# The mask of one attention added by four quarters of TensorE's array, with half of the heads' keys exchanged

## The chip, the cores and the metric

The kernel runs on one core of a Trainium2 chip. The metric is the device time of one execution in microseconds (us). Before the change it is 3333.31 us, the median of three runs (3326.55 to 3346.01). The profile quoted here is of one execution by itself, which took 3340.76 us.

The engines are named as the profile names them: PE is TensorE (matrix products; PEld are its weight loads), DVE is VectorE, ACT is ScalarE, POOL is GpSimd, SP is SyncE, which here issues the DMAs. PSUM is the memory that PE writes; L1050 means line 1050 of the kernel.

## The reference

Two transformer layers on one sequence `x` of 2048 rows by 256 columns, with 16 heads of 16 columns. The first layer has self attention inside each half of the sequence, cross attention between the halves, and an MLP. The second has self attention under a mask over all 2048 keys, cross attention to a context of 1601 rows, and an MLP. Cut to the attention that matters here:

```python
def _mha(q_in, k_in, v_in, qw, qb, kw, kb, vw, vb, ow, ob, mask):
    q = (q_in @ qw + qb).reshape(b, sq, NHEAD, hd).transpose(0, 2, 1, 3)
    k = (k_in @ kw + kb).reshape(b, sk, NHEAD, hd).transpose(0, 2, 1, 3)
    v = (v_in @ vw + vb).reshape(b, sk, NHEAD, hd).transpose(0, 2, 1, 3)
    scores = jnp.einsum('bhqd,bhkd->bhqk', q, k) / jnp.sqrt(jnp.float32(hd))
    if mask is not None:
        scores = jnp.where(mask == 0, jnp.float32(-1000000000.0), scores)
    attn = jax.nn.softmax(scores, axis=-1)
    out = jnp.einsum('bhqk,bhkd->bhqd', attn, v)
    return out.transpose(0, 2, 1, 3).reshape(b, sq, d) @ ow + ob
```

`_mha` runs first with the integer mask (2048 by 2048), then with the context and no mask.

## The kernel before

There are four attention stages, `st` 0 to 3; `st == 2` is the masked one. Queries go by blocks of 512 (`BLK`), heads by groups `g` of four. One group of one block is a unit. Of its four heads two belong to `h` = 0 and two to `h` = 1. In the tiles of keys `kT` and of queries `q` the heads of `h` = 0 lie on partitions 0 to 63 and those of `h` = 1 on 64 to 127, so the score products of the two halves use two different halves of the array's rows. Keys are in slots of 1024 columns, each of eight tiles of 128 keys.

A unit is worked in two passes. The first (`maxima`, L957, L965, L972) computes scores with queries on the partitions and keys along 512 columns, and takes each row's maximum. In the masked stage DVE adds the mask to the scores while it takes the maximum (L965, one instruction for each `h`, followed by a read of its accumulator). The maxima are negated, split into two parts (`negated`) and turned into rows `nm` (`as_rows`, L996).

The second pass (`weights_of`) computes scores with 128 keys on the partitions and 512 queries along the columns (L1035), adds minus the maximum by another pair of products (L1042), and in the masked stage adds the mask, transposed (`bias_columns`, made by `mask_columns` with transposes on PE, L925), by a product with a unit matrix `ident16` (L1050). All three accumulate in one PSUM tile `s_ps` of two banks, a bank for each `h`; ACT then takes the exponential of both banks (L1055). `values_of` multiplies the weights `e` with the values `V`, four heads on four column strips of the array (L1072). `V` has for each key 17 numbers for each head, in the order of the keys.

Both passes take their PSUM tiles from one pool of three (`big_ps`), in turn. The maxima of a unit are computed while the weights of the unit before it are; in the masked stage each step therefore has one pair of products of the maxima, one of weights, and one group of L1072. What else there is to do (MLP, projections, keys and values of the next stage) is cut into pieces and put between the steps by `after` and `evict`. The order of instructions on every engine is the order in which the program issues them (`manual_schedule`). SP issues all DMAs in order: a DMA that waits holds up those behind it. `load_ready` issues one waiting transfer of keys or values a step.

Keys, queries and values are computed once a block (`halves`, `values`). `halves` splits each product in a rounded part `hi` (ACT, L439) and the rest `lo` (DVE, L440), and stores both to DRAM (L444); `c` is the `h` of the heads, `w` is 1 for keys. `values` stores one tile of values by one DMA (L487). The loads back are L809 (keys), L823 (values) and L868 (queries).

Of the kernel before, what the change touches and what calls it, by code (L numbers as in the profile page):

```python
# [12 lines left out]
F32 = mybir.dt.float32  # L13
# [3 lines left out]
AF = mybir.ActivationFunctionType  # L17
ALU = mybir.AluOpType
# [4 lines left out]
P = 128  # L23
# [3 lines left out]
NG = 4  # L27
# [13 lines left out]
GW = 4 * VW  # L41
# [35 lines left out]
def two_layers(ctx: ExitStack, tc: tile.TileContext, a: dict, out: bass.AP):  # L77
    nc = tc.nc
# [74 lines left out]
    ident16 = sb.tile([P, P], BF16, tag="ident16", name="ident16")  # L153
# [37 lines left out]
    def half(shape, dtype=F32, name="half"):  # L191
        return sb.tile(shape, dtype, tag="half", bufs=3, name=name)
# [74 lines left out]
    src = a["cols"][:, :32].rearrange("(c i r) (t w g) -> g i c r t w", c=2, i=2, t=4, w=2)  # L267
    qkb_loads = []
    for g in range(NG):
        for i in range(2):  # L270
            at = (2 * g + i) * HD
# [19 lines left out]
    m = one_ps()  # L291
# [40 lines left out]
    m = one_ps()  # L332
# [48 lines left out]
    def transposed(src, n=BLK, mod=None, tag="hT"):  # L381
# [31 lines left out]
            yield from piece(lambda m, k=k: turn(m, k), lambda m, k=k: take(m, k))  # L413
        return hT

    def halves(st, w, hT, b, n):

        wqk = weights[st][0]
        if w:
            slot = 0 if b in KEYS[st][0] else 1  # L420
            at = KEYS[st][slot].index(b) * BLK
            if (st, slot) not in keys_dr:
                keys_dr[st, slot] = dr.tile([2, 2, P, SLOT], F32, tag="k", bufs=8, name="k_dr")
            d = keys_dr[st, slot][:, :, :, at : at + BLK]
        else:
            d = queries_dr[st, b] = dr.tile(
                [2, 2, P, BLK], F32, tag="q", bufs=4 * NB, name="q_dr"
            )

        def product(m, c):  # L430
            for k in range(2):
                nc.tensor.matmul(  # L432
                    m[:, :n], lhsT=wqk[:, k, w, c, :], rhs=hT[:, k, :n], start=k == 0, stop=k == 1
                )

        def split(m, c):
            hi, lo = half([P, BLK], F32R, name="hi"), half([P, BLK], F32R, name="lo")
            bias = qkb[:, st, w, c : c + 1]
            nc.scalar.activation(hi[:, :n], m[:, :n], AF.Identity, bias=bias)  # L439
            nc.vector.scalar_tensor_tensor(  # L440
                lo[:, :n], m[:, :n], bias, hi[:, :n].bitcast(F32), ALU.add, ALU.subtract
            )
            for i, t in enumerate((hi, lo)):
                nc.sync.dma_start(d[c, i, :, :n], t[:, :n].bitcast(F32))  # L444

        for c in range(2):
            yield from piece(lambda m, c=c: product(m, c), lambda m, c=c: split(m, c))
        if not w:
            done.add(("q", st, b))

    def values(st, hT, b, n):
        _, wv, bv = weights[st]
        t = stage([P, TPB, H * VW], name="v")
        by_head = t.rearrange("p t (h d) -> p t h d", h=H)
        nc.gpsimd.memset(by_head[:, :, :, HD:], 1.0)
        d = dr.tile([P, TPB, H * VW], F32, tag="v", bufs=4 * NB, name="v_dr")
        spans = [(i, min(P, n - i * P)) for i in range((n + P - 1) // P)]

        def product(m, two):
            for j, (i, r) in enumerate(two):  # L460
                for k in range(2):
                    nc.tensor.matmul(  # L462
                        m[:r, j * D : (j + 1) * D], lhsT=hT[:, k, i * P : i * P + r],
                        rhs=wv[:, k, :], start=k == 0, stop=k == 1,
                    )

        def add(m, two):
            full = [i for i, r in two if r == P]
            rest = [i for i, r in two if r < P]
            for r, ii, j in ((P, full, 0), (two[-1][1], rest, len(full))):  # L470
                if ii:
                    nc.vector.tensor_tensor(
                        by_head[:r, ii[0] : ii[0] + len(ii), :, :HD],
                        m[:r, j * D : (j + len(ii)) * D].rearrange(
                            "p (t h d) -> p t h d", t=len(ii), h=H
                        ),
                        along(bv[:r], len(ii), r).rearrange("p t (h d) -> p t h d", h=H),
                        ALU.add,
                    )

        for i in range(0, len(spans), 2):
            two = spans[i : i + 2]
            yield from piece(
                lambda m, two=two: product(m, two), lambda m, two=two: add(m, two)
            )
        full = n // P
        nc.sync.dma_start(d[:, :full, :], t[:, :full, :])  # L487
        if n % P:
            nc.sync.dma_start(d[: n % P, full, :], t[: n % P, full, :])
        values_dr[st, b] = d  # L490

    def keys_and_values(st, hT, b, n=BLK):
        yield from halves(st, 1, hT, b, n + n % 2)
# [438 lines left out]
    def maxima(u):  # L932

        st, b, g = u["st"], u["b"], u["g"]
        masked = st == 2
        chunks = []
        for slot in u["slots"]:
            nk = slot_rows(st, slot)
            n = -(-nk // BLK)
            size = -(-nk // n)  # L940
            size += size % 2
            nk += nk % 2
            chunks += [(slot, c, min(size, nk - c)) for c in range(0, nk, size)]

        def pair(qt, n, i):
            if "pm" not in u:
                load_needed("keys", u)
                u["pm"] = sb.tile([P, TPB, 2, 2, len(chunks)], F32, tag="pm", bufs=2, name="pm")
            if masked and i == 0 and g == NG - 1 and 1 in u["slots"]:
                at = ORDER[2].index(b) + 1  # L950
                each = 2 * 2 // len(chunks)
                for j in range(n * each, (n + 1) * each) if at < NB else ():
                    mask_rows(ORDER[2][at], j // 2, qt, j % 2)
            slot, c, nn = chunks[n]
            s = big_ps()
            for h in range(2):
                nc.tensor.matmul(  # L957
                    s[:, h, :nn],
                    lhsT=u["q"][64 * h : 64 * h + 64, i, qt * P : (qt + 1) * P],
                    rhs=kT[g][slot][64 * h : 64 * h + 64, i, c : c + nn],  # L960
                    start=True, stop=True,
                )
            if masked:
                for h in range(2):
                    nc.vector.tensor_tensor_reduce(  # L965
                        out=s[:, h, :], in0=s[:, h, :],
                        in1=bias_rows[b, slot, qt][:, c : c + nn],
                        scale=1.0, scalar=-3.0e38, op0=ALU.add, op1=ALU.max,
                        accum_out=u["pm"][:, qt, h, i, n : n + 1],
                    )  # L970
            else:
                nc.vector.tensor_reduce(u["pm"][:, qt, :, i, n], s[:, :, :nn], AX.X, ALU.max)  # L972

        return [
            lambda qt=qt, n=n, i=i: pair(qt, n, i)
            for qt in range(TPB) for n in range(len(chunks)) for i in range(2)
        ]
# [43 lines left out]
    def weights_of(u):  # L1021

        st, b, g = u["st"], u["b"], u["g"]
        masked = st == 2
        u["tiles"] = [
            (slot, kt, min(P, slot_rows(st, slot) - kt * P))
            for slot in u["slots"] for kt in range(-(-slot_rows(st, slot) // P))
        ]
        u["e"] = {}

        def pair(n, i):
            slot, kt, r = u["tiles"][n]
            s = big_ps()
            for h in range(2):
                nc.tensor.matmul(  # L1035
                    s[:r, h, :],
                    lhsT=kT[g][slot][64 * h : 64 * h + 64, i, kt * P : kt * P + r],
                    rhs=u["q"][64 * h : 64 * h + 64, i, :],
                    start=True, stop=False,
                )  # L1040
            for h in range(2):
                nc.tensor.matmul(  # L1042
                    s[:r, h, :],
                    lhsT=sel[64 * h : 64 * h + 64, i, :r],
                    rhs=u["nm"][64 * h : 64 * h + 64, :],
                    start=False, stop=not masked,
                )
            if masked:
                for h in range(2):
                    nc.tensor.matmul(  # L1050
                        s[:, h, :], lhsT=ident16, rhs=bias_columns[b, slot, kt],
                        start=False, stop=True,
                    )
            e = u["e"][n, i] = sb.tile([P, 2, BLK], F32, tag="e", bufs=EB, name="e")
            nc.scalar.activation(e[:r], s[:r], AF.Exp, scale=SCALE)  # L1055

        return [lambda n=n, i=i: pair(n, i) for n in range(len(u["tiles"])) for i in range(2)]
# [395 lines left out]
```

## Time and profile before

| what | value |
|---|---|
| median of three runs | 3333.31 us |
| the profiled execution | 3340.76 us |
| its span, first to last instruction | 3338.9 us |
| granted clock of PE over the span | 0.969 |
| mask products, L1050 | 1024, from 1230.2 to 2441.8 us |
| products of the maxima, L957 | 3072, of which 1024 in the masked stage |
| mask and maximum on DVE, L965 | 1024, 701 ns each, and a read of 142 ns |

In rows of groups the columns are line, engine, operation, out<-in with shapes, count, then busy us and the mean ns of one, then idle time of the engine before them and what ended most of it. In the chain of waits each piece has its start, its length, the engine, what it writes and its line. In the timeline the idle time of the engine before a row and its releaser stand in brackets. A tile shape such as 64*128 means 64 rows and 128 columns of the array. The end of a product is modelled.

### The profile page before, as it was taken

To read this page: it belongs to the slowest core of one execution; us is meant where nothing else is said; L and a number is where in the kernel's file an instruction comes from. 1 tells how busy PE (TensorE), PEld (TensorE's weight loads), DVE (VectorE), ACT (ScalarE), POOL (GpSimd) and SP (SyncE) were. 2 spreads that over 40 slices of the span, in tenths; PEclk is the share of its full clock that TensorE was granted. 3 is DMA by queue.
4 is the path that set the end of the run, shared out by engine and by line. 5 is a ranking of instruction groups with operands and counts; after the bars stand their busy time and mean duration, and the time that the engine had idled before them with its cause. 6 is when DMAs were issued, how large, how long until landed. Compare 5 with 4: busy or idle time off the path is not lost.

```text
span 3338.9 us, 56839 instructions
## 1 busy us (share of the span) xinstructions
PE 3054.3 (91%) x22592; PEld 1371.8 (41%) x22592; DVE 2164.9 (65%) x3925; ACT 1718.1 (51%) x1892; POOL 404.0 (12%) x344
## 2 busy tenths in 40 slices
PE   5889999999998989898999999999989999999995
PEld 2434444444444435343433343343344444444433
DVE  4666777775656566566777777777667757666541
ACT  1455565565555545443545555555556546545461
POOL 0001101101011122113013013010010010110102
PEclk8899999999999999999999999999999999999997
DMA  6462251260216121343012011003230100001000
GB/s 171 131 118 80 63 98 58 72 114 26 66 33 116 31 79 42 95 117 101 27 39 59 20 39 52 13 22 70 49 87 27 27 17 21 26 17 27 11 14 16
DMA packets 162363, 191.21 MB, mean 57 GB/s; under 512 B 82584, under 2 KB 95520, under 8 KB 162096
## 3 DMA queue, kind: packets, MB, share of 16 engines
q1 hardware_dynamic: 162096, 187.57, 22.8%
q8 instruction: 178, 2.92, 0.4%
q14 instruction: 89, 0.73, 0.1%
HBM read 129.91 MB, written 48.46 MB: 53 GB/s over the span
## 4 chain that ended last, share of the span: by engine, by line
PE 59%; DVE 6%; ACT 4%; DMA 3%; SPq 2%; issue 2%; POOL 1%; ACTq 0%; POOLq 0%; DVEq 0%
PE m_ps L1072 15%; PE s_ps L1035 10%; PE s_ps L957 9%; PE s_ps L1050 7%; PE s_ps L1042 6%; ACT e L1055 3%; PE m_ps L565 3%; PE m_ps L618 3%; DVE s_ps L965 2%; DVE pm L972 1%; PE m_ps L507 1%; PE m_ps L432 1%; DMA kT<-k_dr 1%; PE m_ps L462 1%; DVE t L375 1%
## 5 line engine op out<-in xcount | busy, mean ns | idle before, releaser
L1055 ACT ACTIVATE e<-s_ps 128x1024 f32<-128x1024 f32 (+1 forms) x1440 | 1466.9, 1024 | 1330.7 <-PE s_ps L1042 739.4
L972 DVE TENSOR_REDUCE pm<-s_ps 128x2 f32<-128x1024 f32 (+3 forms) x1024 | 1122.5, 1107 | 512.2 <-PE s_ps L957 508.9
L1072 PE MATMUL m_ps<-e,V 128*32 128x256 f32 (+2 forms) x10432 | 909.7, 420 | 1.0 <-DVE lo L440 0.8
L965 DVE CUSTOM_DVE_ANT_0 s_ps<-s_ps,bias 128x512 f32<-128x512 f32 x1024 | 713.2, 701 | 286.7 <-PE s_ps L957 147.4
L957 PE MATMUL s_ps<-kT,q 64*128 64x512 f32 (+3 forms) x3072 | 655.5, 428 | 112.4 <-ACT e L1055 63.9
L1035 PE MATMUL s_ps<-q,kT 64*128 64x512 f32 (+1 forms) x2880 | 681.6, 469 | 45.0 <-ACT e L1055 24.7
L1042 PE MATMUL s_ps<-nm,sel 64*128 64x512 f32 (+1 forms) x2880 | 576.2, 395 | 0.0
L957 PEld LDWEIGHTS s_ps<-kT,q 64*128 64x128 f32 x3072 | 295.4, 187 | 475.2 <-issue 244.1
L1035 PEld LDWEIGHTS s_ps<-q,kT 64*128 64x128 f32 (+1 forms) x2880 | 271.5, 185 | 506.9 <-issue 286.6
L1072 PEld LDWEIGHTS m_ps<-e,V 128*32 128x32 f32 (+1 forms) x10432 | 207.2, 109 | 442.6 <-issue 420.7
L1050 PE MATMUL s_ps<-biasT,ident 128*128 128x512 bf16 x1024 | 311.0, 385 | 0.0
L1150 POOL TENSOR_TENSOR oT<-oT,rd_rows 64x512 f32<-64x512 f32 x64 | 81.6, 1275 | 1873.6 <-DMA rd_rows<-rd_dr 1540.2
L1042 PEld LDWEIGHTS s_ps<-nm,sel 64*128 64x128 f32 (+1 forms) x2880 | 277.0, 188 | 10.3 <-ACT nm L1001 0.5
L902 POOL TENSOR_SCALAR bias<-raw 128x512 bf16<-128x512 int32 x64 | 123.0, 1923 | 275.5 <-DMA raw<-in_mask 264.1
L965 DVE DVE_READ_ACCUMULATOR2_ANT pm<- 128x1 f32 x1024 | 145.3, 142 | 0.0
L1050 PEld LDWEIGHTS <-ident 128*128 128x128 bf16 x1024 | 58.3, 97 | 186.4 <-issue 186.4
L432 PE MATMUL m_ps<-hT,w_qk 128*128 128x512 f32 (+2 forms) x224 | 106.6, 599 | 10.4 <-DVE lo L440 7.7
L565 PE MATMUL m_ps<-hT,w_mlp 128*128 128x512 f32 x224 | 110.4, 616 | 5.7 <-ACT sums L1104 4.4
L440 DVE SCALAR_TENSOR_TENSOR lo<-m_ps,qkb,hi 128x512 fp32r<-128x512 f32 (+2 forms) x56 | 41.1, 734 | 109.7 <-ACT hi L439 66.0
L618 PE MATMUL m_ps<-w_mlp,hid 128*128 128x256 f32 x448 | 104.6, 387 | 0.0
L618 PEld LDWEIGHTS m_ps<-w_mlp,hid 128*128 128x128 f32 x448 | 83.9, 191 | 19.3 <-issue 8.5
L462 PE MATMUL m_ps<-w_v,hT 128*128 128x256 f32 (+1 forms) x244 | 63.8, 407 | 25.6 <-DVE lo L440 22.6
(107 smaller groups left out, 1278.0 us busy)
## 6 DMA issues: line engine op xcount, KB each, us to landing
q<-q_dr SPq DMA_DIRECT2D x544, 64.0 KB
kT<-k_dr SPq DMA_DIRECT2D x192, 128.0 KB
raw<-in_mask SPq DMA_DIRECT2D x64, 256.0 KB
q_dr<-hi SPq DMA_DIRECT2D x32, 256.0 KB
q_dr<-lo SPq DMA_DIRECT2D x32, 256.0 KB
oT<-sums SPq DMA_DIRECT2D x256, 32.0 KB
rd_rows<-rd_dr SPq DMA_DIRECT2D x64, 128.0 KB
v_dr<-v SPq DMA_DIRECT2D x14, 544.0 KB
```

Source lines behind the costliest of these rows:

```text
L432: nc.tensor.matmul(m[:, :n], lhsT=wqk[:, k, w, c, :], rhs=hT[:, k, :n], start=k == 0, stop=k == 1)
L565: nc.tensor.matmul(m, lhsT=w1[k][:, f * P : (f + 1) * P], rhs=hT[:, k, :], start=k == 0, stop=k == 1,)
L618: nc.tensor.matmul(m[:, q2 * D : (q2 + 1) * D], lhsT=hid[f][:, qt * P : (qt + 1) * P], rhs=w2[f // 4][:, f % 4, :], start=f == 0, stop=f = ...
L902: nc.gpsimd.tensor_scalar(bias_rows[b, slot, qt][:, j * BLK : (j + 1) * BLK], raw, 0.0, MASKED, ALU.is_equal, ALU.mult,)
L957: nc.tensor.matmul(s[:, h, :nn], lhsT=u["q"][64 * h : 64 * h + 64, i, qt * P : (qt + 1) * P], rhs=kT[g][slot][64 * h : 64 * h + 64, i, c : ...
L965: nc.vector.tensor_tensor_reduce(out=s[:, h, :], in0=s[:, h, :], in1=bias_rows[b, slot, qt][:, c : c + nn], scale=1.0, scalar=-3.0e38, op0 ...
L972: nc.vector.tensor_reduce(u["pm"][:, qt, :, i, n], s[:, :, :nn], AX.X, ALU.max)
L1035: nc.tensor.matmul(s[:r, h, :], lhsT=kT[g][slot][64 * h : 64 * h + 64, i, kt * P : kt * P + r], rhs=u["q"][64 * h : 64 * h + 64, i, :], st ...
L1042: nc.tensor.matmul(s[:r, h, :], lhsT=sel[64 * h : 64 * h + 64, i, :r], rhs=u["nm"][64 * h : 64 * h + 64, :], start=False, stop=not masked,)
L1050: nc.tensor.matmul(s[:, h, :], lhsT=ident16, rhs=bias_columns[b, slot, kt], start=False, stop=True,)
L1055: nc.scalar.activation(e[:r], s[:r], AF.Exp, scale=SCALE)
L1072: nc.tensor.matmul(u["av"][PH * j : PH * (j + 1), cut], lhsT=V[g][slot][:r, kt * GW + j * VW : kt * GW + j * VW + PH], rhs=u["e"][n, j % 2 ...
```

## The change

In the masked stage the mask is added by four products instead of two. Each uses 64 rows and 64 columns of the array: for `h` = 0 the upper and the lower half of the tile of keys go straight (rows 0 to 63 to columns 0 to 63, and 64 to 127 to 64 to 127), for `h` = 1 crossed. For that, the scores of `h` = 1 have the two halves (64 keys each) of every tile of 128 keys exchanged. The exchange is made where keys and values of that stage are stored: `split` writes the keys of `c` = 1 through `exchanged` in two parts, and `values` stores with three DMAs, one for the heads of `h` = 0 and two for those of `h` = 1. In the maxima the mask is in plain order, so there the product of `h` = 1 is made by two products of 256 columns that exchange the keys back.

```diff
+    def exchanged(t, h):
+        return t.rearrange("p (t h x) -> p t h x", h=2, x=P // 2)[:, :, h, :]
...
         def split(m, c):
-            nc.scalar.activation(hi[:, :n], m[:, :n], AF.Identity, bias=bias)
-            nc.vector.scalar_tensor_tensor(
-                lo[:, :n], m[:, :n], bias, hi[:, :n].bitcast(F32), ALU.add, ALU.subtract
-            )
+            if st == 2 and w and c:
+                parts = [(exchanged(m, h), exchanged(hi, 1 - h), exchanged(lo, 1 - h)) for h in range(2)]
+            else:
+                parts = [(m[:, :n], hi[:, :n], lo[:, :n])]
+            for x, high, low in parts:
+                nc.scalar.activation(high, x, AF.Identity, bias=bias)
+                nc.vector.scalar_tensor_tensor(
+                    low, x, bias, high.bitcast(F32), ALU.add, ALU.subtract
+                )
...
+        values_dr[st, b] = d
+        if st == 2:
+            src, dst = (x.rearrange("p t (g c) -> p (t g) c", g=NG) for x in (t, d))
+            nc.sync.dma_start(dst[:, :, : GW // 2], src[:, :, : GW // 2])
+            for at in (0, P // 2):
+                nc.sync.dma_start(
+                    dst[P // 2 - at : P - at, :, GW // 2 :], src[at : at + P // 2, :, GW // 2 :]
+                )
+            return
         nc.sync.dma_start(d[:, :full, :], t[:, :full, :])
...
             for h in range(2):
-                nc.tensor.matmul(
-                    s[:, h, :nn],
-                    lhsT=u["q"][64 * h : 64 * h + 64, i, qt * P : (qt + 1) * P],
-                    rhs=kT[g][slot][64 * h : 64 * h + 64, i, c : c + nn],
-                    start=True, stop=True,
-                )
+                queries = u["q"][64 * h : 64 * h + 64, i, qt * P : (qt + 1) * P]
+                keys = kT[g][slot][64 * h : 64 * h + 64, i, c : c + nn]
+                if masked and h:
+                    for part in range(2):
+                        nc.tensor.matmul(
+                            exchanged(s[:, h, :], part), lhsT=queries,
+                            rhs=exchanged(keys, 1 - part), start=True, stop=True,
+                        )
+                    continue
+                nc.tensor.matmul(s[:, h, :nn], lhsT=queries, rhs=keys, start=True, stop=True)
...
-            if masked:
-                for h in range(2):
-                    nc.tensor.matmul(
-                        s[:, h, :], lhsT=ident16, rhs=bias_columns[b, slot, kt],
-                        start=False, stop=True,
-                    )
+            for h, half_ in ((0, 0), (0, 1), (1, 0), (1, 1)) if masked else ():
+                to, of = 64 * half_, 64 * (half_ ^ h)
+                nc.tensor.matmul(
+                    s[to : to + 64, h, :],
+                    lhsT=ident16[of : of + 64, of : of + 64],
+                    rhs=bias_columns[b, slot, kt][of : of + 64, :],
+                    start=False, stop=True,
+                )
```

More of the change, by code (lines that the diff above doesn't have):

```diff
@@ L489, in values @@
             nc.sync.dma_start(d[: n % P, full, :], t[: n % P, full, :])
-        values_dr[st, b] = d
     def keys_and_values(st, hT, b, n=BLK):
```

## The prediction

> **What bounds the kernel now.** I read the busy table first, then the groups, then the chain of waits and the timeline inside the masked stage. All times are of one profiled execution: span 3338.9 us, its own time 3340.8 us, 0.2% above the median 3333.3 us of the three runs.
>
> ```profile
> PE 3054.3 (91%) x22592; PEld 1371.8 (41%) x22592; DVE 2164.9 (65%) x3925; ACT 1718.1 (51%) x1892; POOL 404.0 (12%) x344
> ```
>
> TensorE is busy 91%. The groups that the change touches or has as neighbours, from the page (line, engine, tile, count, then busy us and mean ns):
>
> ```profile
> L1072 PE MATMUL m_ps<-e,V 128*32 128x256 f32 (+2 forms) x10432 | 909.7, 420 | 1.0 <-DVE lo L440 0.8
> L965 DVE CUSTOM_DVE_ANT_0 s_ps<-s_ps,bias 128x512 f32<-128x512 f32 x1024 | 713.2, 701 | 286.7 <-PE s_ps L957 147.4
> L957 PE MATMUL s_ps<-kT,q 64*128 64x512 f32 (+3 forms) x3072 | 655.5, 428 | 112.4 <-ACT e L1055 63.9
> L1035 PE MATMUL s_ps<-q,kT 64*128 64x512 f32 (+1 forms) x2880 | 681.6, 469 | 45.0 <-ACT e L1055 24.7
> L1050 PE MATMUL s_ps<-biasT,ident 128*128 128x512 bf16 x1024 | 311.0, 385 | 0.0
> ```
>
> Line 1050 is the addition of the mask: 1024 products, two to a step, so 512 masked steps, between 1230 and 2442 us. One such step in the chain of waits of a quiet stretch (start us, us, engine and line):
>
> ```profile
> 2002.38 0.57 PE m_ps L1072 x8
> 2002.95 0.42 PE s_ps L957 x2
> 2003.38 0.26 PE s_ps L1035 x2
> 2003.64 0.23 PE s_ps L1042 x2
> 2003.86 0.54 PE s_ps L1050 x2
> 2004.40 0.57 PE m_ps L1072 x8
> 2004.97 0.43 PE s_ps L957 x2
> 2005.40 0.23 PE s_ps L1035 x2
> ```
>
> The step is five pieces of TensorE work end to end: 0.57 + 0.43 + 0.23 + 0.23 + 0.54 = 2.00 us, and 0.03 more when the L1035 piece is 0.26. The pair of L957 and the pairs of L1035 and L1042 run side by side on the two halves of the rows (each pair takes one stream of 512 columns, 0.23); the two products of L1050 use all rows and follow each other (0.54 = two streams of about 0.22 and about 0.1 around them). What the 0.26 is, the timeline of the same steps tells:
>
> ```profile
> 2002.88 0.19 PEld L957 LDWEIGHTS s_ps<-kT,q 64*128 64x128 f32 x2 [0.41 <-issue]
> 2002.94 0.14 DVE L965 DVE_READ_ACCUMULATOR2_ANT pm<- 128x1 f32 x1
> 2003.13 0.19 PEld L1035 LDWEIGHTS s_ps<-q,kT 64*128 64x128 f32 x2
> 2003.53 0.70 DVE L965 CUSTOM_DVE_ANT_0 s_ps<-s_ps,bias 128x512 f32<-128x512 f32 x1 [0.45 <-ACT e L1055]
> ...
> 2004.94 0.14 DVE L965 DVE_READ_ACCUMULATOR2_ANT pm<- 128x1 f32 x1
> 2005.13 0.19 PEld L1035 LDWEIGHTS s_ps<-q,kT 64*128 64x128 f32 x2
> ```
>
> The weight load of L1035 starts 0.05 us after the DVE read of the maxima ends (2003.08 to 2003.13, 2005.08 to 2005.13): three `s_ps` buffers serve maxima and weights in turn, and L1035 writes the one that DVE has just left. So there is a second loop, over two steps: DVE from its start to its end 1.55 (3.53 to 5.08), 0.05 to the load of L1035, 1.77 from there through L1042, L1050 and L1072 to the L957 after next (5.13 to 6.90), 0.65 from that to the next DVE start. 1.55 + 0.05 + 1.77 + 0.65 = 4.02, or 2.01 a step. TensorE alone (2.00) and this loop (2.01) bind together.
>
> **The mask addition, part by part.** Two products with all rows become four on 64 rows and 64 columns, one on each quarter. If the four stream together, the piece is one stream instead of two. The stream and what surrounds it come from the starts of weight loads: after the first load of L1050, a following load of the same tile shape (line 925) comes at 0.23, as soon as the second stream begins, but that of L1072 at 0.54; so ending the last stream and changing the shape costs 0.54 - 0.23 - 0.22 = about 0.09. Ahead of the stream stands the weight load. For quarter loads no row exists; the nearest are the 128x32 loads of L1072 (load to first column about 0.03: first products last 0.40, later ones 0.38) and the 64x128 loads of L957 (about 0.11: 0.49 against 0.38). I take 0.05 to 0.06, between them in columns. New piece: 0.06 + 0.22 + 0.09 = 0.37 plus 0.01 for four starts (the starts of L1072's four column tiles are 0.006 apart) = 0.38. Saving 0.16 a step. Ends: 0.20 saved if the load is as short as L1072's or shorter; 0.05 lost if only two quarters stream at a time (0.59); 0.48 lost if each goes alone (1.02). I take the first because L1072 shows four column tiles together and L957 two row tiles together.
>
> **The maxima.** For the second half of heads one product of 512 columns becomes two of 256 with the same weights, so 512 extra loads on that row half. The other half still streams 512 columns. First load 0.11, 256 columns 0.11, the second load behind it 0.11, then 256 columns: ready at about 0.34 against 0.33. The nearest row for short products with their own loads is L996 (128 columns): four loads and products start 0.11 apart, so a load hides behind a short product. Taken: +0.01; ends 0 and +0.11 (second load not hidden). DVE waits for the last of the three, so this lies in the DVE loop too.
>
> **A moved wait.** In the changed order of instructions the first L1035 product (line 1061 there) waits for DVE and also for an earlier PE product; the latter is the maxima product that DVE itself waited for, so it is long done, but with two waits the DVE wait becomes an instruction of its own on TensorE's queue. Before shows such ones:
>
> ```profile
> L957 PEldq EVENT_SEMAPHORE x38: 51/51/51, 1747.7 to 2370.6; - x38
> ```
>
> Behind it stand L1035, L1042, the mask and L1072, all in order. Price: 0.05 per step where DVE arrives last, nothing where it is early (TensorE is still streaming L957); ends 0 and 0.11, the distance of two such waits in a row.
>
> **Around them.** Four key splits become two ACT and two DVE instructions of 256 columns in place of one of 512 (0.69 and 0.75 now): under 0.5 us each, four times, beside PE work. Four stores of values turn from one DMA of 128 pieces into three of 4096 pieces of 136 B in all. Their issue on SP:
>
> ```profile
> L823 SPq DMA_DIRECT2D V<-v_dr x64: 387/598/1531, 79.9 to 2473.4; - x64
> L487 SPq DMA_DIRECT2D v_dr<-v x16: 320/338/1192, 73.9 to 1581.1; - x16
> ```
>
> 512 pieces take 0.60, 128 take 0.34: about 0.7 ns a piece more, so about 3.6 us for the three against 0.34. The last of these stores (1359.6) is followed on SP by `kT` loads for which PE waits 8.5 us until 1381.3; between lies a wait of SP for the row maxima until 1371.2, which should swallow the 3 us. Price of all this +3, ends 0 and +13 (four times 3.3, uncovered).
>
> **Sum.** Read from the starts of the mask pairs in order of time, 140 of the gaps between neighbours are over 2.4 us: steps with MLP, projection or other background products on PE (the chain there is TensorE alone, with 1.72 of line 565 in a step of 3.72). The other 372 are quiet steps of 2.0 to 2.2, in most of which the load of L1035 follows DVE by 0.05.
> Quiet: the DVE loop crosses the mask once in two steps: 4.02 - 0.16 + 0.01 + 0.05 = 3.92, 1.96 a step; TensorE alone would be 2.00 - 0.16 + 0.01 = 1.85. DVE's loop wins: gain 0.05 (0.045 unrounded) x 372 = 17 us.
> Heavy: 0.16 - 0.01, and something for waits = 0.137 x 140 = 19 us.
> 17 + 19 - 3 = 33 us: 3340.8 becomes 3308 for a profile of that kind, and the median 3333.3 becomes 3300.
>
> [...] L1035's row tiles write two different banks, L1072's column tiles four partition groups of one bank; no row here has tiles of different rows in one bank. [...]
>
> **Rivals.** (1) Quarters take turns, two at a time: the piece is 0.59, quiet steps lose (0.05 + 0.06) / 2 = 0.06, heavy ones 0.07: 22 + 10 + 3 = +35, 3368. It speaks for it that no row shows four quarters; against, that rows and columns each split well. It decides as soon as the piece exceeds 0.48 (0.38 plus twice the 0.045 that a quiet step gains). Each alone (1.02): (0.48 + 0.06) / 2 x 372 + 0.49 x 140 + 3 = +172, 3505.
> (2) The second load of the maxima is exposed: +0.11 instead of +0.01: quiet steps get 4.02 - 0.16 + 0.11 + 0.05 = 4.02, no gain; heavy ones 0.05 x 140 = 7, less the 3; 3330. Against it stands L996.
> (3) DVE does not bind, because the score products finish in time in both steps or the wait hides: all 512 steps gain 0.14, 70 us, 3266. Against it: 4.02 is added up from four readings that each repeat within 0.02.
>
> **How the numbers follow.** About 0.5% (17 us) can be told from no change. Forecast 0.50 (3290 to 3318), rival 3 0.12, rival 2 with near-nothing outcomes 0.14, rival 1 0.16, slower than that 0.08. Faster by over 0.5%: 0.12 and nearly all of the 0.50, 0.60. Same: 0.16. Slower: 0.24. The range takes in rivals 1 to 3 and leaves out several turns: 3266 to 3368.
>
> **What would show it.** Right: the mask's four products start within 0.03 us of each other and the piece is 0.35 to 0.40; the load of line 1061 follows DVE by about 0.1; quiet steps 1.94 to 1.98, heavy ones 0.14 shorter. Wrong: a mask piece over 0.5; the second maxima product ending 0.1 later; a longer PE gap near 1381 (stores); quiet steps at 1.86 (DVE not binding).

## The result: no change that can be told

After the change the kernel takes 3336.38 us (median of 12 runs, 3329.84 to 3349.09); the kernel before takes 3335.36 us in 12 runs beside it. The ratio is 1.0003, 95% interval 0.9989 to 1.0017. A gain of about 1% was forecast and none came. The profiled execution took 3341.12 us with a span of 3339.3 us, against 3338.9 us before, so the two profiles can be laid over each other.

The mask itself became cheaper. From the busy table and the groups of the kernel after (line, engine, tile, count, busy us and mean ns; L1076 is the mask, L983 the pairs of short products in the maxima of `h` = 1):

```profile
PE 3021.9 (90%) x24128; PEld 1410.7 (42%) x24128; DVE 2164.9 (65%) x3929; ACT 1720.4 (52%) x1896; POOL 404.2 (12%) x344
...
L983 PE MATMUL s_ps<-kT,q 64*128 64x256 f32 x1024 | 252.9, 329 | 9.0 <-DMA kT<-k_dr 8.4
L1076 PE MATMUL s_ps<-biasT,ident 64*64 64x512 bf16 x2048 | 211.3, 403 | 0.0
```

PE is busy 32 us less (3021.9 against 3054.3), in the same span. The chain of waits of the kernel after, in a quiet stretch of the masked stage, shows two steps (L988 is the product of the maxima of `h` = 0, L1061 the scores of the weights):

```profile
2007.91 0.34 PE s_ps L1076 x4
...
2008.83 0.32 PE s_ps L988
2009.14 0.14 PE s_ps L983
...
2009.31 0.50 PE s_ps L1061 x2
...
2010.05 0.34 PE s_ps L1076 x4
...
2011.40 0.23 PE s_ps L1061 x2
...
2011.86 0.34 PE s_ps L1076 x4
```

The mask piece is 0.34 us instead of 0.54: the four quarters run side by side. From one mask to the next is 2.14, then 1.81 us, a mean of 1.97 where it was 2.01. The long step is the one in which L1061 takes 0.50 instead of 0.23. Its weight load, in the timeline of the kernel after, stands behind the DVE read of the maxima:

```profile
2009.02 0.14 DVE L991 DVE_READ_ACCUMULATOR2_ANT pm<- 128x1 f32 x1
2009.28 0.21 PEld L1061 LDWEIGHTS s_ps<-q,kT 64*128 64x128 f32 x2 [0.23 <-PE s_ps L983]
```

The read ends at 2009.16 and the load starts at 2009.28, about 0.12 later, where it was 0.05 before.

So the stage that was changed did gain. From the first to the last mask load it takes 1196.3 us instead of 1211.4. But that first load comes at 1246.9 us instead of 1230.2: the 15.1 us won are lost ahead of the stage, 16.7 us. The ends of the units (the copies of their sums on ACT) tell where. Counted from 0 and against before, unit 21 ends 3.2 us earlier; then units 22, 26 and 30 fall back by 8.2, 10.7 and 5.1 us, each in one jump, and unit 34 by 2.3; between them some 5 us are won back, and no other jump is over 2.6 us. In exactly these four units the stores of values are issued (851.9, 1016.3, 1200.5 and 1375.6 us). At the first of them the chain of waits of the kernel after has one long piece:

```profile
855.27 8.50 DMA q_dr<-hi
...
863.96 0.76 DVE lo L453
...
864.77 0.66 PE m_ps L1022 x4
```

Around it, PE by stretches of 4 us (window, its length, PE busy and instructions, granted clock, mean busy share of the DMA engines, GB/s), kernel after:

```profile
848.00:852.00 4.00, 4.00 (x30) 0.94 0.00 0
852.00:856.00 4.00, 3.95 (x24) 1.00 0.91 89
856.00:860.00 4.00, 3.91 (x26) 1.00 1.51 73
860.00:864.00 4.00, 1.00 (x10) 1.00 0.97 177
864.00:868.00 4.00, 3.23 (x22) 0.69 0.19 69
868.00:872.00 4.00, 4.00 (x36) 0.89 0.20 60
```

and the kernel before, three of the same stretches:

```profile
852.00:856.00 4.00, 4.00 (x28) 1.00 0.36 143
856.00:860.00 4.00, 3.90 (x24) 1.00 0.35 133
860.00:864.00 4.00, 4.00 (x42) 1.00 0.35 131
```

Before, the 128 pieces of the store, of 4352 bytes each, start between 853.4 and 854.7 us in the DMA records, and the stretch that holds them has a share of 0.36. After, the 4096 pieces of 136 bytes start between 853.2 and 860.1 us, at shares of 0.91 and 1.51 and at 89 and 73 GB/s instead of 143 and 133. (The share adds up the times of all pieces; it is over 1 where they overlap.) The store of queries `q_dr<-hi`, issued behind them at 855.27, lands 8.50 us later (in the kernel before it is issued at 855.92, and the last of its pieces and of the `lo` behind it starts at 858.3). Until then DVE may not write a new `lo`, because `hi` and `lo` come from a pool of three buffers (`half`); the products that make the rows `nm` (L1022) wait for this `lo`, and the next unit's weights need `nm`. PE is busy 1.00 of 4 us, and afterwards the granted clock is 0.69 and 0.89 for two windows, by estimate up to 1.7 us more ((0.31 + 0.11) x 4).

### The profile page after: what moved, and what is told of

Same layout as the page of the kernel before. It is cut to its first block, busy times and chain, and to the rows that moved or that the text cites. A ratio compares the mean times of both kernels' runs of the same rounds, so it can differ in the third digit from the quotient of the medians.

```text
span 3339.3 us, 60415 instructions
## 1 busy us (share of the span) xinstructions
PE 3021.9 (90%) x24128; PEld 1410.7 (42%) x24128; DVE 2164.9 (65%) x3929; ACT 1720.4 (52%) x1896; POOL 404.2 (12%) x344
## 4 chain that ended last, share of the span: by engine, by line
PE 58%; DVE 7%; ACT 4%; DMA 3%; issue 2%; SPq 2%; POOL 1%; ACTq 0%; DVEq 0%; POOLq 0%
PE m_ps L1100 15%; PE s_ps L1061 11%; PE s_ps L988 7%; PE s_ps L1068 6%; PE s_ps L1076 4%; ACT e L1083 4%; PE m_ps L587 3%; PE m_ps L640 3%; DVE s_ps L991 3%; PE s_ps L983 2%; PE m_ps L529 1%; DVE pm L998 1%; DMA q_dr<-hi 1%; PE m_ps L475 1%; PE m_ps L439 1%
## 5 line engine op out<-in xcount | busy, mean ns | idle before, releaser
L1061 PE MATMUL s_ps<-q,kT 64*128 64x512 f32 (+1 forms) x2880 | 694.5, 475 | 60.9 <-ACT e L1083 24.5
L988 PE MATMUL s_ps<-kT,q 64*128 64x512 f32 (+3 forms) x2560 | 651.4, 415 | 103.1 <-ACT e L1083 63.9
L1068 PE MATMUL s_ps<-nm,sel 64*128 64x512 f32 (+1 forms) x2880 | 584.0, 396 | 0.0
L1061 PEld LDWEIGHTS s_ps<-q,kT 64*128 64x128 f32 (+1 forms) x2880 | 300.3, 185 | 523.3 <-issue 302.1
L988 PEld LDWEIGHTS s_ps<-kT,q 64*128 64x128 f32 x2560 | 292.9, 187 | 462.8 <-issue 229.5
L1068 PEld LDWEIGHTS s_ps<-nm,sel 64*128 64x128 f32 (+1 forms) x2880 | 284.4, 188 | 2.5 <-ACT nm L1027 0.2
L983 PE MATMUL s_ps<-kT,q 64*128 64x256 f32 x1024 | 252.9, 329 | 9.0 <-DMA kT<-k_dr 8.4
L1076 PE MATMUL s_ps<-biasT,ident 64*64 64x512 bf16 x2048 | 211.3, 403 | 0.0
L983 PEld LDWEIGHTS s_ps<-kT,q 64*128 64x128 f32 x1024 | 152.8, 186 | 11.0 <-issue 10.2
L1076 PEld LDWEIGHTS <-ident 64*64 64x64 bf16 x2048 | 57.9, 103 | 187.5 <-issue 187.5
L453 DVE SCALAR_TENSOR_TENSOR lo<-m_ps,qkb,hi 128x512 fp32r<-128x512 f32 (+3 forms) x60 | 42.0, 699 | 135.6 <-ACT hi L452 64.3
L587 PE MATMUL m_ps<-hT,w_mlp 128*128 128x512 f32 x224 | 111.1, 618 | 5.8 <-ACT sums L1132 4.4
```

What stands on the lines that cost most here:

```text
L587: nc.tensor.matmul(m, lhsT=w1[k][:, f * P : (f + 1) * P], rhs=hT[:, k, :], start=k == 0, stop=k == 1,)
L983: nc.tensor.matmul(exchanged(s[:, h, :], part), lhsT=queries, rhs=exchanged(keys, 1 - part), start=True, stop=True,)
L988: nc.tensor.matmul(s[:, h, :nn], lhsT=queries, rhs=keys, start=True, stop=True)
L1061: nc.tensor.matmul(s[:r, h, :], lhsT=kT[g][slot][64 * h : 64 * h + 64, i, kt * P : kt * P + r], rhs=u["q"][64 * h : 64 * h + 64, i, :], st ...
L1068: nc.tensor.matmul(s[:r, h, :], lhsT=sel[64 * h : 64 * h + 64, i, :r], rhs=u["nm"][64 * h : 64 * h + 64, :], start=False, stop=not masked,)
L1076: nc.tensor.matmul(s[to : to + 64, h, :], lhsT=ident16[of : of + 64, of : of + 64], rhs=bias_columns[b, slot, kt][of : of + 64, :], start= ...
```

## Experiments

All ratios are to the kernel before, run beside the experiment on the same chip. A difference in us is that of the two medians, so it can deviate a little from the ratio, which comes from all runs.

### The stores alone: `store_only`

The kernel before, with only the three stores of `values` from the change (the keys are not exchanged, so half of the heads meet the wrong values).

```diff
+        if st == 2:
+            src, dst = (x.rearrange("p t (g c) -> p (t g) c", g=NG) for x in (t, d))
+            nc.sync.dma_start(dst[:, :, : GW // 2], src[:, :, : GW // 2])
+            for at in (0, P // 2):
+                nc.sync.dma_start(
+                    dst[P // 2 - at : P - at, :, GW // 2 :], src[at : at + P // 2, :, GW // 2 :]
+                )
+            return
```

> The kernel before with the changed store of the masked stage's values alone (three DMAs of 136-byte pieces; keys are not exchanged, so the values of half of the heads meet the wrong keys). Theory S (the stores ate the gain: in the changed kernel the ends of units 22, 26 and 30, each in the time of such a store, are late by 8.2, 10.7 and 5.2 us, of which 16.5 stand at the start of the masked stage): 14 to 20 us slower than before, ratio 1.004 to 1.006, the same three jumps. Theory N (the lag is chance, the masked stage gives nothing): ratio 1.000.

3362.03 against 3335.29 us, ratio 1.0092 (1.0077 to 1.0107): 27 us. The jumps are at the same units: 6.2 us at 22, 7.9 at 26, 7.5 at 30, 3.2 at 34. The waits between 845 and 880 us name the same chain (engine, line and what was waited for: us in total, times, longest):

```profile
DVE lo L440 <- DMA q_dr<-hi: 7.4, 1, 7.4
PEld m_ps L1006 <- DVE lo L440: 4.8, 1, 4.8
```

The stores alone cost more than the change lost, and more than was expected; nothing of the mask is needed for it. Why it is 27 us here and 18 in the changed kernel (next experiment) was not separated.

### The change without its stores: `plain_store`

The kernel after with the one store of before (so the values of half of the heads are not exchanged).

```diff
-        if st == 2:
-            src, dst = (x.rearrange("p t (g c) -> p (t g) c", g=NG) for x in (t, d))
-            nc.sync.dma_start(dst[:, :, : GW // 2], src[:, :, : GW // 2])
...
-            return
```

> The changed kernel with one DMA a block for the values, in the order of the keys (the values of half of the heads are left unexchanged). Theory S: 14 to 20 us faster than before, ratio 0.994 to 0.996, no jumps at units 22, 26, 30. Theory N: ratio 1.000, as the changed kernel.

3318.03 against 3335.29 us, 0.9955 (0.9939 to 0.9972). The units 22 to 34 end within about 2 us of where they end before, and the first mask load comes at 1230.1. So the rest of the change is worth 17 us and the stores take 18 of them.

### The two products and their wait alone: `two_products`

The kernel before, with the maxima of the second half of heads by two products of 256 columns, in plain order.

```diff
-                nc.tensor.matmul(
-                    s[:, h, :nn],
...
+                for x in (0, 256) if masked and h else (None,):
+                    y = slice(0, nn) if x is None else slice(x, x + 256)
+                    nc.tensor.matmul(s[:, h, y], lhsT=queries, rhs=keys[:, y], start=True, stop=True)
```

> The kernel before, with the second half's product of the maxima in two of 256 columns, which also brings the separate instruction that waits for DVE. Keys, values and mask as before. If the wait costs 0.05 us in the DVE loop over two steps and the product 0.01: quiet steps 2.04 instead of 2.01, 372 of them, 8 to 14 us slower, ratio 1.003 to 1.004. If the wait is hidden: ratio 1.000.

3345.95 against 3335.29 us, 1.0037 (1.0024 to 1.005): 11 us. The groups of L1034 (the scores of the weights in this kernel) show the wait as an instruction of its own:

```profile
L1034 PEldq EVENT_SEMAPHORE  x444: 51/51/51, 1189.2 to 2383.5; - x148
```

The kernel before has none there, the kernel after 443 of the same length. In the chain the two products of the maxima (L961) take 0.43 or 0.44 us, as the pair did before, which leaves the wait as what costs: the load of L1034 now starts 0.11 to 0.12 us behind the end of DVE's read in 290 of the 512 steps, where 278 steps of the kernel before have 0.04 to 0.06.

### Values exchanged on PE, maxima by one product: `both`

The kernel after, with both costs removed and the result kept. The values are exchanged when PE makes them: the products for the heads of `h` = 1 write their 64 keys to the other half of the partitions, and the tile is stored by one DMA. The maxima of `h` = 1 are one product whose keys are read with a negative step over the two halves.

```diff
+                    for h, at in ((0, 0), (0, 64), (1, 64), (1, 0)):
+                        to = at if h == 0 else 64 - at
+                        for k in range(2):
+                            nc.tensor.matmul(
+                                y[to : to + 64, :, h, :], lhsT=hT[:, k, i * P + at : i * P + at + 64],
+                                rhs=w[:, k, :, h, :], start=k == 0, stop=k == 1,
+                            )
...
-                    for part in range(2):
...
+                    keys = keys.rearrange("p (t h x) -> p t h x", h=2, x=P // 2)[:, :, ::-1, :]
```

> The changed kernel with the values exchanged where they are computed (products of 64 keys to exchanged partitions, one DMA a block) and the maxima of the second half by one product whose keys are read with a step backwards, so that neither the small pieces nor the extra product nor its wait is there. Theory S: stores give back 17, wait and product 372 x 0.03 = 11, on top of the changed kernel's time; less some 4 us for the value products: 20 to 30 us faster than before, ratio 0.991 to 0.994. Theory N: ratio 0.997 at best, from the wait alone.

3299.28 against 3335.29 us, 0.9895 (0.9881 to 0.991): 36 us faster, more than the 20 to 30 expected. In its chain of waits the maxima are one pair again (L985), and the mask (L1073) is what it was in the kernel after:

```profile
2009.15 0.07 DVE pm L988
2009.22 0.04 issue
2009.26 0.50 PE s_ps L1058 x2
...
2010.90 0.43 PE s_ps L985 x2
...
2011.79 0.34 PE s_ps L1073 x4
```

The scores (L1058) follow the end of DVE by 0.04. The long quiet steps lie mostly between 1.99 and 2.03 us, in the kernel after between 2.08 and 2.16; the short ones are 1.78 to 1.83 in both.

From the first to the last mask load it needs 1173.3 us, 38 less than before, and its first load comes at 1227.4.

### One at a time: `values_pe` and `one_product`

`values_pe` has only the first half of the diff above, `one_product` only the second.

> The changed kernel with the values of the masked stage exchanged where they are computed and stored by one DMA a block; the extra product of the maxima and its wait stay. As plain_store (0.9955) plus 0 to 5 us for the smaller value products: ratio 0.995 to 0.998. If the small products cost more on TensorE than the stores did: ratio 1.000 or over.

> The changed kernel with the maxima of the second half by one product, its keys read with a step backwards, so without the extra product and the separate wait; the stores in small pieces stay. If the wait is worth in the changed kernel what two_products showed against before (12 us): 8 to 16 us faster than before, ratio 0.995 to 0.998. If it is hidden there: ratio 1.000.

`values_pe`: 3319.02 against 3335.39 us, 0.9947 (0.9929 to 0.9965), the same as `plain_store`. So the exchange on PE costs nothing that can be told, and the removed stores are worth 17 us. `one_product`: 3333.49 us, 0.9991 (0.9978 to 1.0004), 3 us better than the kernel after, where 8 to 16 were expected. With the stores away, the same edit is worth 20 us (from `values_pe` to `both`). The profile of `one_product` shows where the gain is: its masked stage takes 1184.6 us, 11.7 less than after, but it begins at 1256.9, 10.0 us later. That execution took 3342.15 us, more than any other of the twelve, and its granted clock is 0.959. The median of the clock over the twelve is 0.9625, against 0.966 for the kernel after and 0.970 for before. Its jumps are at the same four units (10.4, 8.4, 7.3 and 3.2 us), but it is already 4.7 us behind the kernel after at unit 21. Why the time ahead of the stage is longer, where this kernel issues the same work as the kernel after, and whether the clock is its cause, stays open. Single executions scatter by nearly as much: in the eleven profiled kernels that store a block of values by one DMA, the first mask load comes between 1222.1 and 1230.2 us, in the three with small pieces at 1246.9, 1252.8 and 1256.9. The effect of the stores stands out of this scatter; the 10.0 us hardly do.

### Is it the change of tile shape? `late_before` and `late_both`

In the steps with background work the mask saves 0.20 us and the step is no shorter. The chain of waits of the kernel after, with the MLP's first products (L587) as background:

```profile
1315.02 0.23 PE s_ps L1068 x2
1315.25 0.34 PE s_ps L1076 x4
1315.59 1.91 PE m_ps L587 x4
1317.50 0.57 PE m_ps L1100 x8
```

The kernel before, with the same products (L565):

```profile
1284.34 0.23 PE s_ps L1042 x2
1284.58 0.54 PE s_ps L1050 x2
1285.12 1.72 PE m_ps L565 x4
1286.83 0.57 PE m_ps L1072 x8
```

The four background products take 1.91 instead of 1.72. Before, they followed the mask with the same tile shape (128 rows by 128 columns); after, they follow 64 by 64. The theory: the 0.19 is the change of shape. Before, it was paid once, between the background and L1072; now it is paid on both sides of the background. The test puts the background behind the products with `V`, in the kernel before and in `both`: there, in both kernels, background has another shape on both sides.

```diff
                     second[s2]()
+                    if f:
+                        f()
+                        f = None
```

> The kernel before, with the value products directly behind the mask in masked steps, and the background products and transposes behind those. Theory T (a change of tile shape costs 0.2, and before the change background products of the full shape followed a mask of the full shape without one; the quarters put one between them): here each background product pays it, 0.19 in about 100 heavy steps and less in the 64 with transposes: 12 to 30 us slower than before, ratio 1.004 to 1.009. Rival (heavy steps gained nothing for another reason): ratio 1.000.

> The kernel of run both, with the same move of the value products. Theory T: the mask of quarters needs a change of shape behind it anyway, so the move costs nothing: as both, within 6 us, ratio 0.988 to 0.992. If the order alone costs: slower than both by what late_before is slower than before.

`late_before`: 3349.75 against 3337.1 us, 1.0047 (1.003 to 1.0064). Its chain of waits has the 1.91 without any quarters:

```profile
1282.68 0.54 PE s_ps L1050 x2
1283.21 0.57 PE m_ps L1072 x8
1283.78 1.91 PE m_ps L565 x4
1285.70 0.43 PE s_ps L957 x2
```

`late_both`: 3297.63 us, 0.9888 (0.9865 to 0.991), as `both`. In the kernel before the move costs 13 us, in `both`, which already changes shape there, nothing. The steps one by one say the same. From the start of one mask to the start of the next, against the same step of the kernel before (medians, in us; the quiet steps alternate between short and long, so their median is not their mean):

| products between the two masks | steps | kernel after | `late_before` | `late_both` |
|---|---|---|---|---|
| none but those of the step itself | 368 | -0.17 | 0.00 | -0.15 |
| projections or MLP (L432, L462, L507, L565, L618) | 47 | 0.00 | +0.20 | 0.00 |
| transposes of the mask alone (L925) | 58 | -0.08 | +0.10 | -0.09 |
| the rows `nm` (L996) or other transposes (L390) | 35 | 0.00 | +0.16 | -0.01 |

The steps without background work pay nothing for the move, and those with projections or MLP pay 0.20, as much as the quarters save. The 0.19 is thus the neighbour's shape, and not something in the mask.

### Does DVE hold the quiet steps? `short_both` and `short_before`

DVE takes maximum and mask over 384 of the 512 columns (the scale of the exponential is halved, so that no weight overflows; both change the result). Each such DVE instruction (L965 before) then takes 567 instead of 701 ns. The products on PE stay the same.

```diff
+                    w = 384
...
-                        out=s[:, h, :], in0=s[:, h, :],
-                        in1=bias_rows[b, slot, qt][:, c : c + nn],
+                        out=s[:, h, :w], in0=s[:, h, :w],
+                        in1=bias_rows[b, slot, qt][:, c : c + w],
...
+            nc.scalar.activation(e[:r], s[:r], AF.Exp, scale=SCALE / 2 if masked else SCALE)
```

> The kernel of run both, with DVE's pass over the masked scores of the maxima cut to 384 of 512 columns (a quarter of the keys is left out of the maxima, and the exponential of that stage is scaled by a half so that nothing overflows; the output is not the reference's). DVE is shorter by 2 x 0.13 a step. Theory D: the DVE loop falls from 3.82 to 3.55 over two steps, under TensorE's 1.80 a step: quiet steps 1.80 to 1.82 instead of 1.91, 372 x 0.1 = 30 to 40 us faster than both, ratio to before 0.977 to 0.981. If DVE does not hold the steps: as both, 0.9895.

> The kernel before, with the same cut of DVE's pass and of the exponential's scale. Theory D: TensorE's 2.00 stands behind the loop's 2.01, so 0 to 6 us faster, ratio 0.998 to 1.000. If DVE's time counts in any case: as much as in short_both.

`short_both`: 3262.87 against 3335.39 us, 0.9775 (0.9761 to 0.9789), 36 us below `both`. `short_before`: 3317.84 us, 0.995 (0.993 to 0.997), 18 us, where next to nothing was expected. So DVE holds the steps after the change, as forecast; and it held a part of them before as well, more than the two loops of 2.00 and 2.01 us let expect. In the profiled execution the masked stage is 13.8 us shorter (1211.4 to 1197.6 us). Over the 304 quiet steps (at most 2.4 us before, and no products on PE but the step's own) the mean from mask to mask is 2.02 us in the kernel before, 1.99 in `short_before`, 1.93 in `both` and 1.84 in `short_both`.

### Maxima earlier: `early_both` and `early_before`

If DVE holds the steps, its work should start earlier: the products of the maxima go ahead of the mask instead of behind the products with `V`.

```diff
+            if between is not None:
+                between()
...
-                take_maxima(step)
+                if not masked:
+                    take_maxima(step)
...
-                    second[s2]()
+                    second[s2](lambda: take_maxima(step))
```

> The kernel of run both, with the products of the maxima issued between the product that adds the maximum and the mask, instead of ahead of the score product: the same products and as many changes of tile shape, but the way from the score product to the next maxima is shorter by the value products and the mask (0.57 + 0.34). Theory D (after the change quiet steps are held by the DVE loop, 3.82 over two steps, while TensorE needs 1.80): the loop no longer binds, quiet steps 1.80 to 1.85 instead of 1.91, 372 x 0.06 to 0.11 = 22 to 41 us faster than both, ratio to before 0.977 to 0.983. Rival (TensorE or ACT bound): as both, 0.9895.

> The kernel before, with the same move of the maxima and nothing else. Theory D: TensorE needs 2.00 of 2.01, so 0 to 5 us faster, ratio 0.998 to 1.000. If the move itself is what helps: as much as in early_both against both.

Both expectations failed. `early_both` is slower than `both`: 3318.32 against 3337.1 us, 0.9945 (0.9926 to 0.9963). `early_before` is slower than before: 3382.65 us, 1.0146 (1.0125 to 1.0167). The chain of `early_both` tells why:

```profile
2029.84 0.23 PE s_ps L985 x2
2030.07 0.37 PE s_ps L1075 x4
...
2030.52 1.03 ACT e L1082
...
2031.60 0.49 PE s_ps L985 x2
```

The next products of the maxima (L985) need one of the three `s_ps` buffers. With the maxima ahead of the mask, the buffer next in turn is the one whose exponential (L1082, 1.03 us) can start only after the mask. The loop through DVE has become one through ACT. The chain of `early_before` has the same piece of 1.03 us of ACT between the mask and the next maxima.

## Why the prediction was wrong

**Right: the four quarters.** Predicted 0.38 us for the piece, measured 0.34. The four records start 3 to 4 ns apart, also those of the first two quarters, which write different partitions of one bank from different rows of the array. Four streams of about 0.22 us each in 0.34 leave no room for turns.

**Right: the extra product of the maxima.** Predicted +0.01. The two pieces in the chain, 0.32 + 0.12 or 0.14, make 0.44 to 0.46, against 0.43 before.

**Right: the moved wait.** +0.05 was the price; the load of L1061 comes 0.12 behind the end of the DVE read above, and 0.08 to 0.12 behind it in 299 of the 512 steps, against 0.05. Put into the kernel before, it costs 11 us in all (`two_products`).

**Right for a step, too large in the sum: the quiet steps.** 1.96 was predicted, and 1.97 stands in the chain. Over the 366 gaps that were 1.9 to 2.4 us before, the sum is 8 us shorter instead of 17; in `plain_store` it is 14. Most of what lies between 8 and 14 is one gap, at 1384.9 us just behind the fourth store, which grew by 5.1 us and in `plain_store` did not.

**Wrong: "Heavy: 0.16 - 0.01, and something for waits = 0.137 x 140 = 19 us."** These 140 gaps became 6 us shorter in all. In 85 of them (2.4 to 3.0 us before) the mean gain is 0.08 us. The 51 from 3.0 to 6.0 us, most of them with projections or MLP, gained nothing (they are 3.4 us longer in all). The forecast also misread what the 140 are: only 76 have background products on PE. The other 64 have none; 34 of these are long with products of 512 columns of L1072 (1.00 us in the chain instead of 0.57). (Nor are the remaining gaps all 2.0 to 2.2 us: 259 of 371 are.) The 64 gained about what was forecast, 7.7 us (median 0.19), and the 76 gained nothing (median 0.00, 1.4 us longer in all). For the 76, the step took the mask alone from the chain and left its neighbour as it was. The row that should have warned was in the prediction itself: "changing the shape costs ... about 0.09" was taken as part of the mask, but it belongs to the pair of neighbours, and the background had been a neighbour of the same shape.

**Wrong: "Price of all this +3, ends 0 and +13" for the stores.** They cost 18 us (`plain_store`), 27 without the rest of the change (`store_only`). The step priced the issue on SP, and that was right: 0.6 and 0.9 to 1.9 us for the DMAs. It looked for cover there too ("a wait of SP for the row maxima"). What it left out is how long the small pieces keep the DMA engines (at the first store they start over 7.0 us instead of 1.3), what lands late behind them (`q_dr<-hi`, 8.50 us), and who needs its buffer. And it took its cover from the last of the four stores, at 1375.6, where the jump is 2.3 us; the first three make jumps of 24.0 us together.

The sum by these measurements: 15.1 us won in the masked stage (33 + 3 were expected of it), 16.7 lost ahead of it, and 1.2 won behind it: 3338.9 - 15.1 + 16.7 - 1.2 = 3339.3, the span. That `both` gains 36 us, near the forecast of 33, does not make the working right: `both` has the wait and the stores removed, and its 140 heavy gaps are 9 us shorter, not 19. Of the rivals none took place (the bound of 0.48 in the first is 0.47 by its own numbers): no quarters in turns, no exposed load, and `short_both` shows that DVE does hold the quiet steps. The place that decided, the stores, had a term but no rival.

## What to carry to other kernels

A store that is split into short pieces has to be priced at the DMA engines: here, at the first of four stores, 4096 pieces in place of 128 raised their share from 0.36 to 0.91 and 1.51; the four cost 18 us (`plain_store`), and the issue on the queue, 0.6 and 0.9 to 1.9 us for a DMA, said nothing about it. So count pieces, look at the share of the engines while they move, and see which transfers behind them return a buffer. When an instruction gets another tile shape, its two neighbours in time belong to the price: the 0.20 us gained on the mask came back here as 0.19 in the background products behind it. The exchange of rows could be had here from products that run anyway, by where a product writes or in which order it reads (`both`, 36 us faster than before), instead of from a DMA.

## What the runs showed of the hardware

- 4096 pieces of 136 bytes took 7.0 us from the start of the first to the start of the last, with the DMA engines at a busy share of 0.9 to 1.5, and a transfer issued behind them took 8.50 us to land. The same 544 KB as 128 pieces took 1.3 us, at a share of 0.36.
- Two waits of PE were followed by work at a granted clock of 0.50. Windows of the kernel before around one of them (columns as above):

```profile
1168.00:1172.00 4.00, 0.63 (x6) 1.00 0.35 78
1172.00:1176.00 4.00, 0.00 (x0) 0.53 0.30 88
1176.00:1180.00 4.00, 0.05 (x1) 0.50 0.92 309
1180.00:1184.00 4.00, 4.00 (x12) 0.50 0.60 167
1184.00:1188.00 4.00, 4.00 (x22) 0.77 0.15 51
```

  PE is idle from 1168.6 to 1180.0 us. The granted clock falls to 0.50 at 1172.2 and is back at 1.00 at 1185.9, so PE works 5.9 us at 0.50. In the kernel after, the 0.69 and 0.89 behind the 3.8 us of idleness before 864.8 us are 3.4 us at 0.50, from 865.5 to 868.9.
- Four products of 512 columns with a tile of 128 by 128 take 1.72 us behind products of the same shape (kernel before), and 1.91 behind 64 by 64 (kernel after) or 128 by 32 (`late_before`).
- A product whose moving operand is read with a negative step over two halves of 64 columns was no slower in the chain: 0.43 us for the pair in `both` as before.
